# Two attentions and two expert layers in one stream: traced order for loads and gathers, smaller pieces, and another ring of banks for the first attention's turns and projections

## The chip, the core and the metric

The kernel runs on one core of a Trainium2 chip. A core has a matrix engine (TensorE, PE in the profile), a vector engine (VectorE, DVE), a scalar engine for functions of one argument (ScalarE, ACT), a general engine (GpSimd, POOL) and a sync engine (SyncE, SP) from whose queue most DMA transfers are issued. Matrix products land in PSUM, which the kernel uses as eight banks of 128 partitions by 512 floats. The metric is the device time of one execution in microseconds (us), as a median of several runs. A profiled execution, which records every instruction, is longer, and its time is given apart.

## The reference

`x` is 2048 tokens of 128 numbers. Four sublayers are added to it in turn, each fed with a normalization of `x` over its 128 numbers. All is float32.

```
x = x + attention0(layernorm(x))     # 16 heads of 64, all 2048 x 2048 scores, rotary positions
x = x + experts0(layernorm(x))       # 16 experts, the best 2 of 4 groups, the best 4 experts in them
x = x + attention1(layernorm(x))     # 8 heads; each query sees 64 local and 32 chosen positions
x = x + experts1(layernorm(x))       # shared expert + 2 of 8, fixed by the token's number

attention0:  h = layernorm(x) * scale + bias
             q, k, v from two down projections (64 wide) and three up projections; rotary on q and k
             out = softmax(q k^T / 8) v, projected by w_out, + its input
experts0:    s = sigmoid(x Wg); groups by their maximum; weights s / sum(s) * 2.5 of the chosen four
             y = sum_e weight_e * ((silu(x W1_e + b1_e) * (x W3_e + b3_e)) W2_e + b2_e)
attention1:  ckv = x W_dkv (32 wide); index scores I[t,s] = sum_h w_h * relu(qi[t,h] . ki[s])
             idx[t] = the 96 highest of I[t, s <= t], the 64 nearest always among them
             keys, values and a softplus-rotated part are those of ckv and x at idx[t]; softmax over 96
experts1:    y = (shared(x) + (gelu(x W1_a + b1_a) W2_a + gelu(x W1_b + b1_b) W2_b + biases) / 2) / 2
```

## The kernel before

**First attention.** Queries are cut into four groups `g` of 512, heads into eight pairs `pr`; a *unit* is one pair of heads for one group, 32 units in all, group by group. For every unit the scores are computed twice. `by_query` (L264 on) takes 128 queries by 512 keys for both heads: two products `pa` (L275), then a row maximum `mx` on DVE (L280) and exponentials `junk` on ACT (L282) that read the maximum and only keep the row's sum. `close` turns maxima and sums into one reference value and one reciprocal a row, and `turn` (L305 on) transposes the reference values by PE into the row `mrow`. `by_key` (L316 on) computes the transposed scores `pb`, 128 keys by 512 queries (L323), adds the reference by a product of ones with `mrow` (L325), and ACT writes the exponentials `e` (L329). `mean` multiplies them with the compressed values into the accumulator `po` (L338). `project` (L347 on) multiplies `po` with the value and output weights, and DVE adds the result, scaled by the reciprocals, to `xr`, the running `x` of the group.

PSUM is cut into three rings: `ps` with five banks (`pa`, `pb` and the rope's products), `po` with one, `px` with two (all else: `turn`, `project` and everything in the later sublayers). `e` has a ring of seven in SBUF, which the rope's products `t_q`, `t_k` share. `rope` multiplies on DVE (L254) and adds on POOL (L255); keys go to DRAM (`kd`) and come back by two loads a step, `ka` and `kb` (`keys_of`), issued by SP.

**The order.** `run` (L361 on) walks through steps `s`, four to a unit, and in each traces four `by_query`, four `by_key` of the unit before and four `mean` of a step behind that. Between these calls it calls `advance(us)`, 12 us in all in a step. When a group has gone through its eight units, its later sublayers become a *stream*: `follow(g)` is a Python generator that runs `experts0`, `attention1` and `experts1` for the group and yields, after every piece of work, its cost in us. `advance` pulls pieces until their costs have caught up with the time given times `PACE` of that group (L39). So the stream of group `g` is traced between the steps of group `g+1`; the last group's stream has no loop beside it and runs at the end. A stream has about 270 pieces.

Tracing isn't yet the order of execution. A scheduler reorders each engine's instructions by what it takes them to cost and by priority: `mx`, `junk` and `e` are traced with a raised priority (`high_priority(URGENT)`), and `keep_in_program_order` holds single instructions in the order in which they were traced. That order is then fixed for each engine.

**The second attention**, four tiles `n` of 128 queries a group. `index_scores` computes products `pi` of 512 keys (L711), and ACT and DVE build the index scores `v`. `choose` (L733 on) takes the 32 highest of each row by four rounds of maximum, index and replacement on DVE, and turns the indices into `ixT`. Each of 32 *gathers* (L756) then brings one chosen row for 128 partitions from the table in DRAM into `kv`, by an indirect DMA that POOL issues; `pay` (L695) traces them one or a few at a time as the stream's later pieces go by. Eight loads `cl` bring the local windows. `queries` builds the tile's queries. `attend` (L813 on) first rotates the gathered rows, two halves of 16 slots each, four DVE instructions a half (`rotate`, L90 on; the first of them is `rgc`, L95), transposes them (L831), computes scores `pl` (L849 to L855), maximum (L861), exponentials (L865), transposes, and the products with values and output weights (L886 to L907). Slot `2 (g mod 16) + g div 16` takes gather `g`, so the first half holds gathers 0 to 7 and 16 to 23. The tiles are strung together like this:

```
for n in range(4 * g, 4 * g + 4):
    yield from index_scores(n)
    while gathers:
        yield pay(1.8)
    yield from choose(n)
    if pending is not None:
        yield from attend(*pending)
    yield from queries(n)
    pending = (n, self.kv, self.cl, *self.qT)
```

so `attend` of a tile is traced when the next tile has been chosen, and the last one after its own gathers. Both gathers and the multiplications of the gathered rows' rotation are kept in program order.

Of the kernel before, what the change touches and what calls it, by code (L numbers as in the profile page):

```python
# [16 lines left out]
P = 128  # L17
# [21 lines left out]
PACE = (1.0, 1.1, 1.2, 1.2)  # L39
# [24 lines left out]
def layernorm(nc, pool, src, dst, tag):  # L64

    nt = src.shape[1]
    st = pool.tile([P, nt, 6], F32, tag=tag + "st", name=tag + "st")
    mv = pool.tile([P, nt, 2], F32, tag=tag + "mv", name=tag + "mv")
    for n in range(nt):
        nc.vector.bn_stats(st[:, n, :], src[:, n, :])  # L70
        nc.vector.bn_aggr(mv[:, n, :], st[:, n, :])
    v = pool.tile([P, nt], F32, tag=tag + "v", name=tag + "v")
    nc.vector.tensor_scalar(v, mv[:, :, 1], EPS, None, ALU.add)
    r = rsqrt(nc, pool, v, tag)
    for n in range(nt):
        nc.vector.tensor_scalar(
            dst[:, n, :], src[:, n, :], mv[:, n, 0:1], r[:, n : n + 1], ALU.subtract, ALU.mult
        )


def softplus(nc, pool, out, src, one, tag):

    a = pool.tile(list(out.shape), F32, tag=tag + "a", name=tag + "a", bufs=1)
    nc.scalar.activation(a, src, AF.Abs)
    nc.scalar.activation(a, a, AF.Exp, scale=-1.0)
    nc.scalar.activation(a, a, AF.Ln, bias=one)
    nc.vector.scalar_tensor_tensor(out, src, 0.0, a, ALU.max, ALU.add)


def rotate(nc, eng, pool, out1, out2, mu, cos, sin, tag, bufs=None, keep=None):  # L90

    shape = list(mu.shape)
    c = pool.tile(shape, F32, tag=tag + "c", name=tag + "c", bufs=bufs)
    s = pool.tile(shape, F32, tag=tag + "s", name=tag + "s", bufs=bufs)
    first = eng.tensor_tensor(c, mu, bcast(cos, 2, 2), ALU.mult)  # L95
    if keep is not None:
        keep(first)
    second = eng.tensor_tensor(s, mu, bcast(sin, 2, 2), ALU.mult)
    if keep is not None:
        keep(second)  # L100
    eng.tensor_tensor(out1, c[:, :, 0, :], s[:, :, 1, :], ALU.subtract)
    eng.tensor_tensor(out2, s[:, :, 0, :], c[:, :, 1, :], ALU.add)


class Program:
# [23 lines left out]
    def bank(self, name):  # L129

        return self.ps_s.tile([P, 512], F32, tag="ps", name=name)
# [5 lines left out]
    def transposed(self, src, dst, name):  # L137

        pt = self.x(name)
        for j in range(4):  # L140
            self.nc.tensor.transpose(pt[:, j, :], src[:, j, :], self.ident)
        self.nc.scalar.copy(dst, pt.rearrange("p a b -> p (a b)"))

    def prologue(self):
# [40 lines left out]
        for g in range(4):  # L187
            cols = slice(512 * g, 512 * g + 512)
            xn = pp.tile([P, 4, C], F32, tag="xn", name=f"xn{g}", bufs=2)
            layernorm(nc, pp, self.xr[g], xn, "ln0")  # L190
            nc.gpsimd.tensor_tensor(self.xr[g], self.xr[g], xn, ALU.add)
            hn = pp.tile([P, 4, C], F32, tag="hn", name=f"hn{g}", bufs=2)
            layernorm(nc, pp, xn, hn, "ln0")
# [33 lines left out]
        self.ep = self.ctx.enter_context(tc.tile_pool(name="a_e", bufs=7))  # L227
# [77 lines left out]
    def turn(self, u):  # L305

        nc = self.nc
        pm = self.x(f"pt{u}", dtype=BF16)
# [38 lines left out]
    def project(self, u, h):  # L347
# [4 lines left out]
        pm = self.x(f"pp{u}_{h}")  # L352
# [8 lines left out]
    def run(self):  # L361
# [26 lines left out]
        for s in range(4 * NU + BEHIND + 5):  # L388
            u, j = divmod(s, 4)
            ub, jb = divmod(s - BEHIND, 4)  # L390
            um, jm = divmod(s - BEHIND - 1, 4)
            if u < NU and j == 0 and u + 1 < NU:
                self.rope(self.UNITS[u + 1][0], "q", self.UNITS[u + 1][1])
            if u + 1 < 8:
                self.rope(u + 1, "k", j)
            if s == 4 * 8:
                self.keys.close()
            if s + 2 < 4 * NU:
                self.keys_of((s + 2) // 4, (s + 2) % 4, "a")
            sb = s + 2 - BEHIND  # L400
            if 0 <= sb < 4 * NU:
                self.keys_of(sb // 4, sb % 4, "b")
            for half in range(2):
                pair = range(2 * half, 2 * half + 2)
                for i in pair:
                    if 0 <= ub < NU:
                        self.by_key(ub, 4 * jb + i)
                    advance(1.0)
                    if u < NU:
                        self.by_query(u, 4 * j + i)  # L410
                    advance(1.0)
                if half == 1 and u < NU and j == 3:
                    self.close(u)
                for i in pair:
                    if 0 <= um < NU:
                        self.mean(um, 4 * jm + i)
                if half == 0 and j == 0 and 0 <= u - 1 < NU:
                    self.turn(u - 1)
                advance(2.0)
                if jm == 1 and 0 <= um - 1 < NU:  # L420
                    self.project(um - 1, half)
            if jm == 1 and 0 <= um - 1 < NU:
                self.outs.pop(um - 1)
                if um % 8 == 0:
                    if stream is not None:
                        for _ in stream:
                            pass
                    stream, owed, pace = self.follow(um // 8 - 1), 0.0, PACE[um // 8 - 1]
        if stream is not None:
            for _ in stream:  # L430
                pass
# [86 lines left out]
    def experts0(self, sc, g):  # L518
# [6 lines left out]
        layernorm(nc, sm, xr, xn, "ln1")  # L525
        yield 5.0
        xT = sm.tile([P, 512], F32, tag="xT", name=f"xT1_{g}")
        self.transposed(xn, xT, f"pt1_{g}")
        yield 2.0
# [4 lines left out]
        for j in range(4):  # L534
            nc.tensor.matmul(pg[:, j, :], xT[:, j * P : j * P + P], w["wg"], start=True, stop=True)
        s = sm.tile([P, 4, NE0], F32, tag="s", name=f"gs{g}")
# [4 lines left out]
        yield 2.0  # L541
# [3 lines left out]
        def below(v, n, first, k, tag):  # L545
# [3 lines left out]
            eq = sm.tile(shape, F32, tag="eq", name=f"eq{tag}{g}")  # L549
            nc.vector.tensor_tensor(gt, bcast(v, 2, n), bcast(v, 3, n), ALU.is_gt)  # L550
            nc.vector.tensor_tensor(eq, bcast(v, 2, n), bcast(v, 3, n), ALU.is_equal)
            ff = bcast(first.rearrange("p a b -> p (a b)"), 1, 4)
            e2 = eq.rearrange("p t a b -> p t (a b)")
            nc.vector.tensor_tensor(e2, e2, ff, ALU.mult)
            nc.vector.tensor_tensor(gt, gt, eq, ALU.add)
            rank = sm.tile([P, 4, n], F32, tag="rank" + tag, name=f"rank{tag}{g}")
            nc.vector.tensor_reduce(rank, gt, axis=AX.X, op=ALU.add)
            nc.vector.tensor_scalar(rank, rank, float(k) - 0.5, None, ALU.is_lt)
            return rank
# [4 lines left out]
        gsel = below(gm, NG0, w["first4"], 2, "g")  # L564
        yield 3.0
# [6 lines left out]
        esel = below(ms, NE0, w["first16"], 4, "e")  # L572
        yield 7.0
# [13 lines left out]
        yield 2.0  # L587

        pt = self.x(f"ptw{g}", [P, P])
        nc.tensor.transpose(pt, we.rearrange("p a b -> p (a b)"), self.ident)  # L590
        wt = sm.tile([P, P], F32, tag="wt", name=f"wt{g}")
        nc.scalar.copy(wt, pt)
        yield 1.0
        pb = self.x(f"pb2_{g}")
        nc.tensor.matmul(pb.rearrange("p a b -> p (a b)"), wt, w["b2"], start=True, stop=True)
        nc.vector.tensor_tensor(xr, xr, pb, ALU.add)
        yield 1.5


        hs = {}  # L600
        for e in range(NE0 + 1):
            if e < NE0:
                if e + 2 < NE0:
                    wx.append(self.weights(wp, e + 2, f"wb{g}_{e + 2}"))
                hs[e] = self.hidden(hp, wx[e], xT, w["b13"][:, 0, e : e + 1], self.hb[:, e : e + 1], w["b13"][:, 1, e : e + 1], f"b{g}_{e}")
                yield 2.0
            if e > 0:
                h = hs.pop(e - 1)
                py = self.x(f"py{g}_{e}")
                for j in range(4):  # L610
                    nc.tensor.matmul(py[:, j, :], h[:, j * P : j * P + P], wx[e - 1][:, 2, :], start=True, stop=True)
                yield 1.0
                for j in range(4):
                    nc.vector.scalar_tensor_tensor(
                        xr[:, j, :], py[:, j, :], wh[:, j, e - 1 : e], xr[:, j, :], ALU.mult, ALU.add
                    )
                yield 1.0

    def hidden(self, pool, wx, xT, b1, hb1, b3, name):

        nc = self.nc
        p1, p3 = self.x("p1" + name, [P, 512]), self.x("p3" + name, [P, 512])
        nc.tensor.matmul(p1, wx[:, 0, :], xT, start=True, stop=True)  # L623
        nc.tensor.matmul(p3, wx[:, 1, :], xT, start=True, stop=True)  # L624
# [4 lines left out]
        h = pool.tile([P, 512], F32, tag="h", name="h" + name)  # L629
        nc.vector.scalar_tensor_tensor(h, th, 1.0, z, ALU.add, ALU.mult)  # L630
        nc.vector.scalar_tensor_tensor(h, p3, b3, h, ALU.add, ALU.mult)  # L631
        return h

    def attention1(self, sc, g):
# [12 lines left out]
        with ExitStack() as prep:  # L647
            pp = prep.enter_context(tc.tile_pool(name="c_prep", bufs=1, side="right"))
            xn = pp.tile([P, 4, C], F32, tag="xn", name=f"xn2_{g}")
            layernorm(nc, pp, xr, xn, "ln2")  # L650
            yield 5.0
            xT = pp.tile([P, 512], F32, tag="xT", name=f"xT2_{g}")
            self.transposed(xn, xT, f"pt2_{g}")
            yield 2.0
# [3 lines left out]
            for j in range(4):  # L658
                nc.tensor.matmul(pk[:, j, :], xT[:, j * P : j * P + P], w["wck"], start=True, stop=True)
            kg = pp.tile([P, 4, 64], F32, tag="kg", name=f"kg{g}")  # L660
            nc.scalar.copy(kg[:, :, 0:32], pk[:, :, 0:32])
            softplus(nc, pp, kg[:, :, 32:64], pk[:, :, 32:64], self.one, "spk")
            nc.sync.dma_start(table.rearrange("(n p) d -> p n d", p=P)[:, 4 * g : 4 * g + 4, :], kg)
            yield 3.0
# [451 lines left out]
```

## Time and profile before

| | us |
|---|---|
| three runs | 3023.91, 3023.21, 3025.91 (median 3023.91) |
| the profiled execution | 3467.66 |
| its span, first to last instruction | 3465.9 |
| PE busy in the span | 2798.2 (81%) |
| ACT busy | 1739.4 (50%) |
| DVE busy | 1715.1 (49%) |
| POOL busy | 577.9 (17%), of it 491.0 in gathers |
| mean clock granted to PE | 0.861 of full speed |

How to read it: a busy time is the time in which an engine executes instructions; "idle before" is what it stood before a group of instructions, with the event that ended most of that idle time. A line such as `mx<-pa` gives the output and input by the program's names, buffer numbers left out. The clock is a share of full speed. The profiled execution is 443.8 us longer than the median of the runs, so what the profile shows is not all there when nothing is recorded. Before the loop's first `pa` lie 77.8 us of preparation; the loop ends at 2899.7 and the last group's stream at 3465.9. In that tail the last tile's `attend` runs from 3395.9 to 3427.2, and `choose` of tile 12 ends at 3048.0.

### The profile page before, as it was taken

How to read it: one execution, taken by the hardware profiler on the slowest of the kernel's cores; microseconds unless marked ns; L12 is line 12 of the kernel's file. 1: busy time of each engine (PE TensorE's matmuls, PEld its weight loads, DVE VectorE, ACT ScalarE, POOL GpSimd, SP SyncE). 2: the span in 40 equal slices, each digit the busy share in tenths (PEclk: the TensorE clock that was granted, in tenths of full speed). 3: DMA queues.
4: the chain of work that ended last, by engine and by line, in shares of the span. 5: the costliest groups of instructions: out<-in, count | busy, mean ns of one | idle time of the engine just before them, and what ended most of it. 6: DMA issues, size and time to landing. Idle time of an engine off the chain costs nothing. (4 is left out here: it accounts for less than half of the span.)

```text
span 3465.9 us, 38526 instructions
## 1 busy us (share of the span) xinstructions
PE 2798.2 (81%) x13452; PEld 1256.3 (36%) x13452; DVE 1715.1 (49%) x3749; ACT 1739.4 (50%) x4157; POOL 577.9 (17%) x586
## 2 busy tenths in 40 slices
PE   5999999998788899997697899997696877733426
PEld 3444444343233344442243344342242333312214
DVE  7645444565343444665363545555354624664242
ACT  2766667565464566564464466564363542312213
POOL 1111100002313210002312300002303210061330
PEclk7999999999797799998897899997797978856556
DMA  4211111111111111111111111111111101010000
GB/s 130 64 52 52 59 49 38 37 45 33 34 37 27 31 52 38 41 39 28 32 39 28 30 49 43 39 35 28 31 29 25 23 12 42 24 21 5 14 12 26
DMA packets 98097, 127.74 MB, mean 37 GB/s; under 512 B 31344, under 2 KB 49776, under 8 KB 97904
## 3 DMA queue, kind: packets, MB, share of 16 engines
q1 hardware_dynamic: 81520, 108.48, 11.1%
q0 software_dynamic: 16384, 16.81, 2.4%
q8 instruction: 106, 1.74, 0.2%
q14 instruction: 87, 0.71, 0.1%
HBM read 115.26 MB, written 9.96 MB: 36 GB/s over the span
## 5 line engine op out<-in xcount | busy, mean ns | idle before, releaser
L280 DVE TENSOR_REDUCE mx<-pa 128x1 f32<-128x512 f32 x1024 | 673.2, 686 | 695.7 <-PE pa L275 502.3
L282 ACT ACTIVATE junk<-pa,mx 128x512 bf16<-128x512 f32 x1024 | 699.9, 691 | 423.2 <-DVE mx L280 384.5
L275 PE MATMUL pa<-ka,q 64*128 64x512 f32 x2048 | 777.8, 639 | 87.7 <-ACT junk L282 68.2
L329 ACT ACTIVATE e<-pb 128x512 f32<-128x512 f32 x1024 | 556.5, 597 | 473.2 <-PE pb L325 356.2
L323 PE MATMUL pb<-q,kb 64*128 64x512 f32 x2048 | 693.4, 646 | 99.6 <-ACT e L329 73.1
L756 POOL DMA_INDIRECT kv<-table,ixT x512 | 491.0, 959 | 926.1 <-issue 484.2
L338 PE MATMUL po<-e,ckv 128*64 128x512 f32 x2048 | 552.0, 659 | 1.7 <-issue 1.7
L275 PEld LDWEIGHTS pa<-ka,q 64*128 64x128 f32 x2048 | 272.5, 193 | 351.7 <-ACT junk L282 190.3
L323 PEld LDWEIGHTS pb<-q,kb 64*128 64x128 f32 x2048 | 233.7, 193 | 350.9 <-issue 165.6
L255 POOL TENSOR_TENSOR q<-t_q 128x512 f32<-128x512 f32 x32 | 40.7, 1273 | 1560.7 <-DVE t_q L254 1560.7
L325 PE MATMUL pb<-mrow,onesb 64*128 64x512 bf16 x1024 | 262.8, 386 | 2.0 <-issue 1.9
L338 PEld LDWEIGHTS po<-e,ckv 128*64 128x64 f32 x2048 | 133.9, 146 | 348.9 <-issue 337.3
L282 ACT ACTIVATION_READ_ACCUMULATOR junk<-pa,mx 128x1 f32 x1024 | 209.2, 204 | 0.0
L861 DVE TENSOR_REDUCE mx<-pl 128x2 f32<-128x416 f32 x64 | 37.8, 591 | 343.7 <-remote 158.0
L865 ACT ACTIVATE e<-pl,mx 128x208 f32<-128x208 f32 x128 | 54.4, 431 | 242.6 <-DVE mx L862 173.7
L711 PE MATMUL pi<-kiT,qiT 64*128 64x512 f32 (+4 forms) x320 | 123.9, 632 | 47.3 <-issue 17.9
L831 PE MATMUL ptr<-ident,kv 128*128 128x128 f32 x256 | 44.3, 315 | 94.7 <-issue 66.9
L855 PE MATMUL pl<-kr,qT 64*32 64x128 f32 x1024 | 66.9, 320 | 63.6 <-issue 63.5
L325 PEld LDWEIGHTS <-onesb 64*128 64x128 bf16 x1024 | 75.6, 96 | 112.2 <-issue 90.3
L717 DVE SCALAR_TENSOR_TENSOR v<-rl,iw_sb,v 128x512 f32<-128x512 f32 (+4 forms) x120 | 77.1, 644 | 71.9 <-ACT rl L716 64.2
L832 ACT COPY kr<-ptr 128x512 f32<-128x512 f32 x64 | 37.0, 590 | 142.7 <-PE ptr L831 97.0
L630 DVE SCALAR_TENSOR_TENSOR hb<-thb,zb 128x512 f32<-128x512 f32 x64 | 44.3, 692 | 129.4 <-ACT zb L628 127.4
(266 smaller groups left out, 2856.4 us busy)
## 6 DMA issues: line engine op xcount, KB each, us to landing
ka<-kd SPq DMA_DIRECT2D x128, 256.0 KB
kb<-kd SPq DMA_DIRECT2D x128, 256.0 KB
wb<-in_wx SPq DMA_DIRECT2D x64, 192.0 KB
kd<-kst SPq DMA_DIRECT2D x32, 256.0 KB
kv<-table,ixT POOLq DMA_INDIRECT x512
wd<-in_wx SPq DMA_DIRECT2D x40, 192.0 KB
csk<-in_cs SPq DMA_DIRECT2D x4, 512.0 KB
csq<-in_cs SPq DMA_DIRECT2D x4, 512.0 KB
```

Source lines behind the costliest of these rows:

```text
L275: nc.tensor.matmul(ps[h], q[rows, qt * P : qt * P + P], k[rows, :], start=True, stop=True)
L280: nc.vector.tensor_reduce(mx[at], ps[h], axis=AX.X, op=ALU.max, negate=True)
L282: nc.scalar.activation(junk, ps[h], AF.Exp, bias=mx[at], accum_out=su[at])
L323: nc.tensor.matmul(ps[h], k[rows, c], q[rows, :], start=True, stop=False)
L325: nc.tensor.matmul(ps[h], self.onesb[rows, :], mrow[rows, :], start=False, stop=True)
L329: nc.scalar.activation(e[:, h, :], ps[h], AF.Exp)
L338: nc.tensor.matmul(self.pos[u][cols, :], self.ckv[:, kb, :], e[:, h, :], start=(kb == 0), stop=(kb == NT - 1))
L711: nc.tensor.matmul(pi[:, : hi - lo], qiT[h // 2][rows, q], kiT[rows, lo:hi], start=True, stop=True)
L717: nc.vector.scalar_tensor_tensor(v[:, lo:hi], rl[:, : hi - lo], w["iw"][:, h : h + 1], v[:, lo:hi], ALU.mult, ALU.add)
L756: nc.gpsimd.indirect_dma_start(out=kv[:, 2 * (g % 16) + g // 16, :], out_offset=None, in_=table[0 : P * (n + 1), :], in_offset=bass.Indire ...
L855: nc.tensor.matmul(pl[32 * j : 32 * j + 32, c, 80:NK], qs[rows, 32 * gr : 32 * gr + 32], kr[rows, gr % 16, :], start=False, stop=(c == 1),)
L865: nc.scalar.activation(e[:, i, :], pl[:, c, :], AF.Exp, scale=SCALE1, bias=mx[:, i : i + 1], accum_out=su[:, i : i + 1],)
```

## The change

- `manual_schedule` over the engines SP and POOL: both issue their instructions in the order in which they are traced; loads and gathers are no longer placed by the scheduler. `keep_in_program_order` around gathers and rotations goes.
- The later sublayers are cut into more pieces, about 450 a group by the generators' yields, mostly a matrix product or its eviction each. `layernorm`, `softplus`, `rotate`, `transposed` and `hidden` become generators. In `hidden` the product `p3` is traced after the evictions of `p1`, and an expert's output product and addition are traced within the next expert's pieces. `index_scores` is traced so that additions come one piece after the relu that they read. `e` in `attend` is scaled in two halves. `PACE` falls, and a step still advances by 12 us.
- One gather is traced with every piece of `queries` and the following `index_scores` (`paced`). `attend` of a tile and `choose` of the next are merged, one piece of each in turn.
- `turn` and `project` take their banks from the ring of five instead of the ring of two. The ring of `e` has eight buffers.

```diff
-PACE = (1.0, 1.1, 1.2, 1.2)
+PACE = (0.86, 0.93, 1.0, 1.0)
...
-def rotate(nc, eng, pool, out1, out2, mu, cos, sin, tag, bufs=None, keep=None):
+def rotate(nc, pool, out1, out2, mu, cos, sin, tag):
...
+    nc.vector.tensor_tensor(c, mu, bcast(cos, 2, 2), ALU.mult)
+    yield us
+    nc.vector.tensor_tensor(s, mu, bcast(sin, 2, 2), ALU.mult)
+    yield us
+    nc.vector.tensor_tensor(out1, c[:, :, 0, :], s[:, :, 1, :], ALU.subtract)
+    nc.vector.tensor_tensor(out2, s[:, :, 0, :], c[:, :, 1, :], ALU.add)
+    yield us
+
+
+def merge(*parts):
+
+    parts = list(parts)
+    while parts:
+        for p in list(parts):
+            us = next(p, None)
+            if us is None:
+                parts.remove(p)
+            else:
+                yield us
...
-    def bank(self, name):
-
-        return self.ps_s.tile([P, 512], F32, tag="ps", name=name)
+    def bank(self, name, shape=(P, 512), dtype=F32):
+
+        return self.ps_s.tile(list(shape), dtype, tag="ps", name=name)
...
-        self.ep = self.ctx.enter_context(tc.tile_pool(name="a_e", bufs=7))
+        self.ep = self.ctx.enter_context(tc.tile_pool(name="a_e", bufs=8))
...
-        pm = self.x(f"pt{u}", dtype=BF16)
+        pm = self.bank(f"pt{u}", [P, 4, P], BF16)
...
-        pm = self.x(f"pp{u}_{h}")
+        pm = self.bank(f"pp{u}_{h}", [P, 4, C])
...
+        with self.tc.manual_schedule(engines={mybir.EngineType.SP, mybir.EngineType.Pool}):
+            for s in range(4 * NU + BEHIND + 5):
...
+                    for i in pair:
+                        if 0 <= um < NU:
+                            self.mean(um, 4 * jm + i)
+                        advance(1.0)
...
+        last = iter(())
+        for e in range(NE0):
...
+            for k, _ in enumerate(self.hidden(hp, wx[e], xT, *bias, f"b{g}_{e}", h)):
+                if k in (1, 2):
+                    next(last, None)
+                yield 0.8
+            last = output(e, h)
...
-        p1, p3 = self.x("p1" + name, [P, 512]), self.x("p3" + name, [P, 512])
+        p1 = self.x("p1" + name, [P, 512])
         nc.tensor.matmul(p1, wx[:, 0, :], xT, start=True, stop=True)
-        nc.tensor.matmul(p3, wx[:, 1, :], xT, start=True, stop=True)
+        yield
...
+        p3 = self.x("p3" + name, [P, 512])
+        nc.tensor.matmul(p3, wx[:, 1, :], xT, start=True, stop=True)
+        yield
...
-        def pay(us):
-
-            for _ in range(min(len(gathers), max(1, round(us / 1.8)))):
-                gathers.pop(0)()
-            return us
+        def paced(pieces):
+
+            for us in pieces:
+                if gathers:
+                    gathers.pop(0)()
+                yield us
...
-                    tc.keep_in_program_order(
-                        nc.gpsimd.indirect_dma_start(
-                            out=kv[:, 2 * (g % 16) + g // 16, :], out_offset=None, in_=table[0 : P * (n + 1), :],
-                            in_offset=bass.IndirectOffsetOnAxis(ap=ixT[:, g : g + 1], axis=0),
-                        )
+                    nc.gpsimd.indirect_dma_start(
+                        out=kv[:, 2 * (g % 16) + g // 16, :], out_offset=None, in_=table[0 : P * (n + 1), :],
+                        in_offset=bass.IndirectOffsetOnAxis(ap=ixT[:, g : g + 1], axis=0),
                     )
...
-        pending = None
+        last = iter(())
         for n in range(4 * g, 4 * g + 4):
-            yield from index_scores(n)
+            yield from paced(index_scores(n))
             while gathers:
-                yield pay(1.8)
-            yield from choose(n)
-            if pending is not None:
-                yield from attend(*pending)
-            yield from queries(n)
-            pending = (n, self.kv, self.cl, *self.qT)
+                yield from paced(iter((0.8,)))
+            yield from merge(choose(n), last)
+            yield from paced(queries(n))
+            last = attend(n, self.kv, self.cl, *self.qT)
         while gathers:
-            yield pay(1.8)
-        yield from attend(*pending)
+            yield from paced(iter((0.8,)))
+        yield from last
```

## The prediction, made before the changed kernel had been run

> **What bounds the kernel now.** I read the page first (busy times, 40 slices, groups), then busy time by stretch, then the waits and the timeline where the stretches lose time.
>
> From the page of the kernel before:
>
> ```profile
> span 3465.9 us, 38526 instructions
> PE 2798.2 (81%) x13452; PEld 1256.3 (36%) x13452; DVE 1715.1 (49%) x3749; ACT 1739.4 (50%) x4157; POOL 577.9 (17%) x586
> ...
> PEclk7999999999797799998897899997797978856556
> ...
> L756 POOL DMA_INDIRECT kv<-table,ixT x512 | 491.0, 959 | 926.1 <-issue 484.2
> ```
>
> TensorE (PE) is the busiest engine. Its clock is full in the first quarter and falls in three dents and in the last seventh. The 512 gathers take POOL 959 ns each.
>
> Busy time by stretch: a bare stretch of three units, one beside `experts0`, two beside `attention1`, and the tail after the loop (columns: us, then busy us and count per engine):
>
> ```profile
> core 0: us, PE busy (x) PEld busy (x) DVE busy (x) ACT busy (x) POOL busy (x), PEclk, DMA share, GB/s
> 454.90:625.30 170.40, 170.40 (x747) 71.85 (x745) 78.91 (x154) 120.21 (x297) 3.81 (x3) 1.00 0.14 38
> 714.10:797.40 83.30, 83.30 (x379) 37.12 (x376) 53.46 (x139) 55.06 (x123) 1.26 (x1) 1.00 0.15 40
> 889.50:991.20 101.70, 77.98 (x441) 33.48 (x438) 36.09 (x72) 48.95 (x125) 32.56 (x34) 0.83 0.13 32
> 2613.50:2653.50 40.00, 18.22 (x90) 7.60 (x87) 6.35 (x13) 7.11 (x16) 30.26 (x32) 0.72 0.18 39
> 2899.70:3465.90 566.20, 263.79 (x1384) 152.24 (x1383) 260.23 (x485) 121.95 (x261) 122.61 (x128) 0.63 0.08 19
> ```
>
> The bare units are bound by PE: 170.4 of 170.4 us, 56.8 a unit, 3.55 for each of the 16 key blocks. Beside `experts0` PE is still full. Beside `attention1` it is busy 78 of 102 us, and 18 of 40 in a stretch full of gathers, at clock 0.72. The tail (566 us) is a chain of latencies, PE busy under half.
>
> Now how a gather holds everything. Tile 8 is the one tile where the second rotation (`rgc`, L95) came up on VectorE (DVE) before its last gathers. Timeline there (start, duration, then in brackets the idle time before):
>
> ```profile
> 2446.35 0.96 POOL L756 DMA_INDIRECT kv<-table,ixT  x1
> ...
> 2456.48 0.69 DVE L95 TENSOR_TENSOR rgc<-kv,cs 128x512 f32<-128x512 f32 x1 [10.38 <-DMA kv<-table,ixT]
> ...
> 2457.87 0.69 ACT L282 ACTIVATE junk<-pa,mx 128x512 bf16<-128x512 f32 x1 [9.92 <-DVE mx L280]
> ...
> 2458.70 1.22 PE L275 MATMUL pa<-ka,q 64*128 64x512 f32 x1 [6.94 <-issue]
> ```
>
> DVE stood 10.38 us in front of an instruction that waited for gathers; everything behind it stood too, `mx` (L280) first, so ACT lacked `mx`, kept its banks, and PE lost 6.94. So PE rides out 3.4 us of a held DVE, then stops. The last gather needed ended at 2454.9, the rotation began at 2456.5: 1.6 us to land. Gathers start every 1.25 us (2446.35, 2447.62 and so on). The waits (us, times, of which at most in one):
>
> ```profile
> DVE rgc L95 <- DMA kv<-table,ixT: 20.0, 3, 10.4
> ```
>
> Three such cases in all, 20.0 us: first rotations of tiles 0 and 4, second of 8. All others came late enough.
>
> A second thing happens where some twenty gathers have run without a break:
>
> ```profile
> 1676.49 0.95 POOL L756 DMA_INDIRECT kv<-table,ixT  x1 [0.30 <-issue]
> ...
> 1696.51 0.94 POOL L756 DMA_INDIRECT kv<-table,ixT  x1 [0.30 <-issue]
> 1701.29 0.60 ACT L329 ACTIVATE e<-pb 128x512 f32<-128x512 f32 x1 [25.11 <-remote]
> ```
>
> All engines stand, no local releaser is named ("remote"), and go on 4 us after the last gather. The profiled execution took 3467.66 us (span 3465.9), the runs 3023.91: 443.8 us or 27.7 for each of 16 tiles. I take this freeze as the profiler's and absent in the runs.
>
> [...]
>
> **The change, part by part.** The instructions are the same, but for 16 DVE multiplies more (`e` scaled in halves: [...] beside PE work but for the tail: 0). Cost is in order and waits. The orders below are those of the two built programs.
>
> *1. Gathers out of the scheduler's hands, `attend` merged with the next `choose`.* Before, `attend(n)` is traced after `choose(n+1)`; from tile n's index transpose to its first rotation DVE has 21 to 58 maxima over `pa` in tiles 0 to 10. In the changed program, from a tile's first gather to its first rotation DVE has only 4, 4, 5, 4, 4, 6, 6, 6, 5 (tiles 0, 1, 4, 5, 7 to 11): mean 4.9, two to a key block, so 2.45 x 3.55 = 8.7 us of the loop, and some 3 us of stream matmuls among them: 12 us. The first rotation needs gathers 0 to 23 (slots under 16): 24 x 1.25 + 1.6 = 31.6 us. It waits 19.6, PE loses 19.6 - 3.4 = 16.2; nine tiles: 146. The second needs all 32: 41.6. From the first, 10 us later; one key block and the rotation's 2.2 us lie between, it waits 4, of which I count 2 on PE: 18. Tiles 2, 3 and 6 have `q`'s addition (L255) between their gathers. After it 7 gathers are owed in tile 2 (11.6 us with the addition, PE loses 5, and 16 earlier), in tile 3 19 for the first rotation (26.6, less 7 reached and 3.4: 16, and 2), in tile 6 4, then 12 (3 in all): 42. Sum 206. The waits of before (20.0 us, PE about 10) go: +196. Queued behind the waiting rotation: `mx`, then ACT's exponentials, then PE's banks. Bounds: +100 if DVE arrives only 20 us after the first gather, +270 if after 6.
>
> *2. Clock after each of some twelve stops.* [...] +20 (10 to 40).
>
> *3. Tail.* Before, one after the other: `attend` 31 us (tile 15: 3395.9 to 3427.2), `queries` 10, scores 16 to 20, `choose` 24; gathers under `attend`. Now `choose` runs within `attend` (24 + 8 us of DVE), but for tile 13 both rotations stand before the scores of tile 14 on DVE, and `attend` cannot start before its gathers. From `choose(12)`'s end to the kernel's: before 19 + 23, three times (31 + 10), scores 16 + 20, `choose` 24 + 26, 31 and the last stage's 39: 321. After: `choose(13)` ends at 69 (rotation at 42 + 3, then 24 of DVE), gathers to 111, scores to 130, `choose(14)` 162, gathers to 204, scores 212, `choose(15)` 244, gathers 286, `attend` 29, last stage 39: 354. The difference is +33; I take +25 (-35 to +45), as fewer eviction waits help elsewhere.
>
> *4. Smaller pieces, matmul and eviction apart, `px` banks for the streams alone, an `e` ring of 8.* Removes waits in `attention1`. In the profile PE idles 330 us between 625 and 2900; about 190 us of standstill and slow clock are left if I take PE busy time by clock (2367 us with the prologue) from the end of the loop in the runs (3024 - 468, the tail without freezes). `experts0` has nothing to give (PE full). I take a third: -60 (-20 to -130).
>
> *5. `turn` and `project` in the ring of five.* Three more tenants a unit, each held about 3 us (matmul 1.2, four DVE steps 1.1, wait), where `pa` and `pb` hold 3.4 banks on average: +5 (0 to +40).
>
> *6. Loads on SP in traced order.* `ka`, `kb` are traced two steps, 28 us, ahead; an issue takes 0.33 us. What SP queues before them, `cl` and `wx`, waits for matmuls traced earlier: 0, covered by those two steps; uncovered, a key load late by 5 us would cost PE 5 in each of 12 tiles (+60). Lower `PACE`: streams end at step 70, 102, 134 against 69, 101, 133, before the next starts: 0.
>
> Sum: 196 + 20 + 25 - 60 + 5 = +186; 3023.9 + 186 = 3210. In the profile's own account 3467.7 + 186 = 3654, less what waits and freezes share, since both end with the gathers: some 8 us by tile, about 3550.
>
> **Rivals.** *A, the forecast* (3110 to 3310). For it: the case at 2456.5 and the counts of maxima. Against: only three cases in a trace. *B, the freeze is real in the runs too*: the new waits then fall into time already lost; 196 shrinks to about 60, 3024 + 60 + 20 + 25 - 60 + 5: 3075. Against: 443.8 us between profile and runs. *C, faster*: without the profiler the gathers issue quickly. Then 24 of them must be down within the 12 us that DVE needs, one every (12 - 1.6)/24 = 0.43 us; below that no rotation waits, parts 1 and 2 give -10, the tail gains two thirds of three `choose`s (-50), the pieces -60: 2905. Against: 1.25 us at every one of 490 spacings, quiet or busy. *D, no effect* (the scheduler restores the old order): excluded by the orders, but sums can cancel.
>
> **How the numbers follow.** A 0.68, B 0.16, C 0.14, D 0.02. The time is A's. The range reaches from B's side to part 1's upper bound: 3050 to 3330, leaving out C and 2 in 100 above. A measurement of this kernel can tell about 0.2% from no change. Slower 0.83 (A and most of B), same 0.03, faster 0.14.
>
> **What would show it.** Right: `rgc` waits for the `kv` gathers by about 20 us in nine tiles and 4 more at their second rotation, some 200 to 250 us in the chain of waits against 20.0; PE idle "pa" behind it; tile 13's scores after its gathers. Wrong: rotations that wait little; `attention1` units shorter than before; a tail under 500 us with no waits; new idle on `pa` for key loads.

## The result, and the profile after

The changed kernel takes 3359.84 us (median; 3355.55 to 3364.83), the kernel before 3023.56: a ratio of 1.1104, 95% interval 1.1086 to 1.1123. The profiled execution took 3364.83 us. The prediction was 3210, range 3050 to 3330: the direction held, but the time lies 30 us above the range, and the loss of 336 us is nearly twice the 186 that were forecast.

The page of the changed kernel, the lines that answer to those shown of before:

```profile
span 3363.0 us, 38462 instructions
PE 2748.0 (82%) x13452; PEld 1216.9 (36%) x13452; DVE 1702.8 (51%) x3765; ACT 1732.6 (52%) x4157; POOL 575.7 (17%) x586
...
PEclk6999999999888989999779889999879779875556
...
L819 POOL DMA_INDIRECT kv<-table,ixT x512 | 489.0, 955 | 705.0 <-issue 351.9
...
L103 DVE TENSOR_TENSOR rgc<-kv,cs 128x512 f32<-128x512 f32 x32 | 22.3, 696 | 415.7 <-DMA kv<-table,ixT 415.7
```

The first multiplication of a rotation, `rgc`, now waits 415.7 us for gathers, in all 32 rotations; it was 20.0 us in three (22.7 in four in e14). The gathers themselves are as they were (955 ns against 959).

The profile of before in the first part turned out to be a bad ruler: it comes from an execution in which the other engines slowed down or stood while gathers ran, and the timed runs were not like that (see e1 and e14). That a profiled execution is longer, as the first part says, hardly holds here: in e14 it takes 3026.74 us beside a median of 3021.99. e14 profiled the kernel before on a chip where it takes these 3022 us. Busy time there in the loop from the first unit that has a stream beside it, and in the tail (us of the stretch, then busy us and count of each engine, clock, DMA):

```profile
core 0: us, PE busy (x) PEld busy (x) DVE busy (x) ACT busy (x) POOL busy (x), PEclk, DMA share, GB/s
624.90:2557.60 1932.70, 1832.55 (x9576) 813.22 (x9571) 1106.59 (x2456) 1222.05 (x2931) 395.76 (x405) 0.96 0.15 40
2557.60:3025.00 467.40, 258.20 (x1384) 150.44 (x1383) 260.58 (x485) 122.31 (x261) 127.36 (x128) 0.65 0.09 23
```

The same two stretches of the changed kernel, same columns:

```profile
635.50:2862.50 2227.00, 1869.69 (x9500) 790.11 (x9495) 1095.50 (x2461) 1213.52 (x2923) 392.17 (x405) 0.90 0.13 35
2862.50:3363.00 500.50, 279.85 (x1460) 163.55 (x1459) 259.27 (x495) 129.13 (x270) 123.43 (x128) 0.63 0.09 21
```

This is where the 338 us between the two profiled executions (3363.0 and 3025.0) lie. The loop is 294.3 us longer: PE's idle time there went from 100.2 to 357.3 (+257), and its busy time from 1832.6 to 1869.7 (+37), at a mean clock of 0.90 against 0.96. The tail is 33.1 longer; 76 matrix products more lie in it than before (1460 against 1384). The remaining 10.6 lie before that unit. The other trace of the changed kernel, e5, reaches the unit at 624.3 us, as early as before, so this part is put down to the one execution.

How one tile loses it: tile 4, timeline of the changed kernel.

```profile
1588.03 0.96 POOL L819 DMA_INDIRECT kv<-table,ixT  x1 [16.56 <-DMA cl<-table]
...
1600.18 1.94 PE L364 MATMUL po<-e,ckv 128*64 128x512 f32 x8
...
1619.61 0.69 DVE L103 TENSOR_TENSOR rgc<-kv,cs 128x512 f32<-128x512 f32 x1 [23.16 <-DMA kv<-table,ixT]
...
1620.99 0.69 ACT L308 ACTIVATE junk<-pa,mx 128x512 bf16<-128x512 f32 x1 [22.72 <-DVE mx L306]
...
1623.28 2.07 PE L754 MATMUL pi<-kiT,qiT 64*128 64x512 f32 x2 [21.15 <-ACT qT L871]
...
1629.70 0.69 DVE L103 TENSOR_TENSOR rgc<-kv,cs 128x512 f32<-128x512 f32 x1 [7.38 <-DMA kv<-table,ixT]
...
1633.67 1.22 PE L754 MATMUL pi<-kiT,qiT 64*128 64x512 f32 x1 [8.32 <-ACT qT L871]
```

VectorE comes to the rotation at 1596.4 (1619.61 less the wait), 8.4 us after the first gather's start (1588.0), and stands 23.16 us. PE goes on until 1602.1 with what it has, then stands 21.15. Ten us later the second rotation waits 7.38 for the last eight gathers, and PE stands 8.32 behind it. Over the twelve tiles of the loop the first rotations wait 254 us and the second ones 82.

### The profile page after: what moved, and what is told of

The parts are those of the page before. It is cut to its first block, busy times and chain, and to the rows that moved or that the text cites. A ratio compares the mean times of both kernels' runs of the same rounds, so it can differ in the third digit from the quotient of the medians.

```text
span 3363.0 us, 38462 instructions
## 1 busy us (share of the span) xinstructions
PE 2748.0 (82%) x13452; PEld 1216.9 (36%) x13452; DVE 1702.8 (51%) x3765; ACT 1732.6 (52%) x4157; POOL 575.7 (17%) x586
## 5 line engine op out<-in xcount | busy, mean ns | idle before, releaser
L301 PE MATMUL pa<-ka,q 64*128 64x512 f32 x2048 | 741.2, 637 | 176.2 <-ACT junk L308 169.6
L349 PE MATMUL pb<-q,kb 64*128 64x512 f32 x2048 | 637.1, 639 | 33.2 <-ACT junk L308 18.8
L301 PEld LDWEIGHTS pa<-ka,q 64*128 64x128 f32 x2048 | 257.0, 192 | 440.6 <-ACT junk L308 290.1
L349 PEld LDWEIGHTS pb<-q,kb 64*128 64x128 f32 x2048 | 215.4, 190 | 274.5 <-issue 117.6
L351 PE MATMUL pb<-mrow,onesb 64*128 64x512 bf16 x1024 | 245.0, 383 | 0.0
L103 DVE TENSOR_TENSOR rgc<-kv,cs 128x512 f32<-128x512 f32 x32 | 22.3, 696 | 415.7 <-DMA kv<-table,ixT 415.7
L867 PE MATMUL ptq<-ident,qq 128*128 128x128 f32 x256 | 47.7, 331 | 90.5 <-ACT qT L871 46.0
L383 DVE SCALAR_TENSOR_TENSOR xr<-pp,rs,xr 128x128 f32<-128x128 f32 x256 | 72.8, 344 | 72.7 <-PE pp L380 72.7
L754 PEld LDWEIGHTS pi<-kiT,qiT 64*128 64x128 f32 x320 | 52.2, 231 | 143.5 <-DVE v L773 50.8
L759 ACT ACTIVATE rl<-pi 128x512 f32<-128x512 f32 (+4 forms) x120 | 58.7, 516 | 84.3 <-PE pi L754 72.9
```

The costliest lines, as they stand in the source:

```text
L301: nc.tensor.matmul(ps[h], q[rows, qt * P : qt * P + P], k[rows, :], start=True, stop=True)
L349: nc.tensor.matmul(ps[h], k[rows, c], q[rows, :], start=True, stop=False)
L351: nc.tensor.matmul(ps[h], self.onesb[rows, :], mrow[rows, :], start=False, stop=True)
L383: nc.vector.scalar_tensor_tensor(xr[:, j, :], pm[:, j, :], self.rs[u][:, j, h : h + 1], xr[:, j, :], ALU.mult, ALU.add)
L754: nc.tensor.matmul(pi, qiT[h // 2][rows, q], kiT[rows, lo:hi], start=True, stop=True)
L759: nc.scalar.activation(rl, pi, AF.Relu)
```

## The experiments

The chips were not alike. On some, the kernel before takes 3023 us, as in the comparison; on others its median is 3428 to 3455. Each run below is set against the kernel before on its own chip, and that time is given. "A chip that slows" means one of the second kind.

**Theory 1:** the loss is VectorE standing before rotations that were placed ahead of their gathers. **Theory 2:** the smaller pieces, the banks or SP's order make it. **Theory 3:** the gathers hold the chip, wherever VectorE stands.

**e1, e14: the kernel before, profiled again.**

> The kernel before, unchanged, profiled once more. If the 443.8 us between its profiled execution and its runs are what recording costs, the new span is again near 3460 us with all engines standing for 14 to 25 us behind long rows of gathers. If that one execution was a disturbed one, the span is near 3022 us, the engines go on during the gathers, and the loop ends near 2560 us instead of 2899.7. The profiled execution of the changed kernel, whose span (3363.0) is its own run's time, speaks for the second.

> The kernel before, for its profile. If it runs at about 3023 us here, the loop ends near 2560 us, PE is near 100% beside gathers, and no engine stands in rows of gathers except for VectorE before three rotations; the tail takes about 465 us.

Measured: e1 3446.3 us, and 3449.18 (15 runs) for the kernel before beside it; e14 3021.99, beside 3024.77. So the long execution in the first part was no effect of recording, since e14 is recorded too and spans 3025.0 us; nor a single disturbance, since e1's chip shows it in every run. It goes with the chip, or with the hour, since each chip was seen in one session only. Away from gathers the two kinds are alike: the first unit with a stream beside it begins at 624.9 us in e14 and at 625.3 in the first profile, in which gathers slow PE too. The same row of 32 gathers (the last nine of tile 4 and 23 of tile 5), busy times in e14:

```profile
1530.20:1569.50 39.30, 38.05 (x174) 15.42 (x173) 16.86 (x28) 26.81 (x66) 29.83 (x32) 1.00 0.21 53
```

and in e1:

```profile
1650.70:1690.50 39.80, 16.87 (x59) 5.56 (x55) 6.66 (x11) 9.10 (x23) 30.20 (x33) 0.73 0.16 39
```

With the gathers going at the same pace, PE does 38.05 us of work in 39.3 on the one chip and 16.87 in 39.8 on the other. The timeline of e1 within another row shows PE's instructions coming slowly one by one, with no event that they would wait for ("issue"):

```profile
1165.63 0.18 PEld L323 LDWEIGHTS pb<-q,kb 64*128 64x128 f32 x1 [1.53 <-issue]
...
1166.35 0.37 PE L325 MATMUL pb<-mrow,onesb 64*128 64x512 bf16 x1
...
1167.76 0.10 PEld L325 LDWEIGHTS <-onesb 64*128 64x128 bf16 x1 [1.82 <-issue]
1168.46 0.58 PE L325 MATMUL pb<-mrow,onesb 64*128 64x512 bf16 x1 [1.70 <-issue]
```

**e2, e7, e13: the changed kernel with the rotations held.**

```diff
-    nc.vector.tensor_tensor(c, mu, bcast(cos, 2, 2), ALU.mult)
+    keep(nc.vector.tensor_tensor(c, mu, bcast(cos, 2, 2), ALU.mult))
...
-    nc.vector.tensor_tensor(s, mu, bcast(sin, 2, 2), ALU.mult)
+    keep(nc.vector.tensor_tensor(s, mu, bcast(sin, 2, 2), ALU.mult))
```

`keep` is `tc.keep_in_program_order` for the gathered rows and nothing elsewhere.

> The changed kernel, with the two multiplications of each rotation of gathered rows held in program order again, as before. In the order of instructions their place moves from 4 to 34 maxima behind the index transpose to 8 to 46, which is where PE's transposes of the rows want them. Theory 1 (VectorE standing before gathers makes the loss): the waits of rgc for gathers fall from 415.7 us to under 130 (the tail's 80 stay) and the time from 3360 to about 3080 us (3020 to 3140). Theory 2 (smaller pieces, banks or SP's order make the loss): above 3290. Theory 3 (the gathers themselves hold the chip, wherever VectorE stands): above 3290 too, with waits moved to other instructions.

> The changed kernel with the rotations held, once more, to be set against the unchanged one on one chip. Where gathers don't slow the others, theory 1 gives 2960 to 3080 us (the plain load gave 2943) and theory 2 (pieces, banks, SP's order) above 3290; where they do, it stays near 3470 as in the first run of it, since nothing but the place of the loss is changed.

> The changed kernel with real gathers and the rotations held in program order. If before runs at about 3023 us here, theory 1 gives 2960 to 3050 (stand-ins with the hold gave 3019, the plain load 2943), with waits of rgc under 40 us in the loop; theory 2 over 3250. If before runs at about 3450, about 3475 as in its first two runs.

Measured: e2 3472.68 us beside 3449.18 (ratio 1.0063, 1.0043 to 1.0083), e7 3477.11 beside 3454.79 (1.0082, 1.0049 to 1.0114), both on chips where gathers slow PE. e13, on one where they don't: 3041.22 beside 3024.77 (1.0052, 1.0034 to 1.0071), as theory 1 expected. Where gathers leave PE alone, the hold gives back 319 of the 336 us. On a chip that slows it gives nothing back: e7 is 29 us longer than the unheld kernel on the same chip (e5, below). Waits of the rotations in e13 (us, times, longest):

```profile
DVE rgc L103 <- DMA kv<-table,ixT: 67.4, 9, 12.7
```

Of these, 34 us lie in the loop, where it was 336. The two stretches of e13, to be set against those of the changed kernel above; the number of products in each is the same:

```profile
623.80:2563.60 1939.80, 1828.93 (x9500) 770.24 (x9496) 1094.60 (x2461) 1212.83 (x2923) 400.40 (x405) 0.96 0.15 40
2563.60:3027.20 463.60, 259.89 (x1460) 154.76 (x1459) 259.20 (x495) 128.22 (x270) 125.80 (x128) 0.67 0.09 23
```

Without the waits the loop is 287 us shorter: PE is idle for 110.9 instead of 357.3 and busy for 1828.9 instead of 1869.7, and the tail is 37 shorter. The loop's mean clock is 0.96 (0.90 in the changed kernel, 0.96 in e14). So the hold takes away the lost clock and the tail's loss as well as the idle time.

In the order of instructions one sees why. The table counts the maxima `mx` on VectorE and the products `pa` on PE from the start of the loop, two to a key block:

| tile | index transpose after maximum | first rotation, changed | first rotation, held | PE's transposes after product |
|---|---|---|---|---|
| 0 | 392 | 396 | 400 | 412 |
| 4 | 648 | 653 | 660 | 670 |
| 5 | 664 (held 668) | 676 | 704 | 710 |
| 9 | 928 (held 930) | 934 | 960 | 970 |

PE's transposes stand at the same place in both kernels. Nobody needs the rotated rows before them, so the early rotations served nothing. If the merge of `choose` and `attend` alone is undone in the changed program, tile 4's 5 maxima and tile 9's 6 between index transpose and rotation stay as they are. It is the dropped hold, not the merge, that moved them. (That is its order alone; it was not run.)

**e3, e4: one plain load in place of a tile's gathers.**

```diff
-            gathers.extend(gather(g) for g in range(32))
+            nc.sync.dma_start(
+                kv.rearrange("p r d -> p (r d)"),
+                table[0:RK, :].rearrange("r d -> (r d)").unsqueeze(0).to_broadcast([P, RK * 64]),
+            )
```

> The changed kernel, with the 32 gathers of a tile replaced by one plain load of 32 fixed rows to all partitions from SP; the choice of rows is left out of what is computed, all other work stays. Theory 1: no rotation waits over 5 us in the loop, the loop's loss and the tail's 80 us of waits go, and the time is about 2970 us (2880 to 3060). Theory 2: the loop keeps its loss, only the tail gains some 60: about 3290 us. Theory 3: about 2970 as in theory 1, so the next kernel tells 1 and 3 apart.

> The kernel before, with the same replacement of the gathers; the choice of rows is left out of what is computed. Theory 1: gathers cost the kernel before little, the three waits of 20 us and part of those in the tail: 2960 us (2920 to 3010). Theory 3: gathers hold the kernel before as well: under 2880.

Measured, both on a chip that slows: the changed kernel 2942.89 us (2935.89 to 2947.85), the kernel before 3012.17 (3007.28 to 3013.68; 2 us above what was expected), beside 3449.18. All that such a chip adds hangs on the gathers: 437 us for the kernel before. On the other chips its gathers cost some 12 us (3024 against 3012), those of the changed kernel some 417 (3360 against 2943), if the kernels with the plain load take as long there. Without gathers the changed kernel is faster by 69 us on one chip, of which 66 lie in the tail (392.8 us after the loop against 459.0) and 5 in the loop (1921.7 against 1927.1).

**e5, e6, e8, e19: on chips that slow.** e5 is the changed kernel as it is; e6 and e19 are the kernel before without the hold of the rotations (`tc.keep_in_program_order` dropped from the call); e8 is the changed kernel with `self.x` for `self.bank` in `turn` and `project`.

> The changed kernel, unchanged, beside the kernel before on whatever chip this is. The last runs gave 3449 us for the kernel before where the comparison had 3023.6, and the profile shows PE at two thirds while gathers run; in the profile of the changed kernel PE was full beside 20 gathers (24.70 of 24.70 us, clock 1.00). If the gathers of this chip slow the other engines (before at about 3450), the waits of the changed kernel fall into time that is lost anyway: 3360 to 3480. If they don't (before at about 3023), 3360 as before.

> The kernel before, with nothing changed but that the rotations of gathered rows are no longer held in program order. In the order of instructions, tiles 8 to 11 then have 5, 10, 6 and 6 maxima between index transpose and rotation (21, 54, 39, 6 before), the others 15 to 44. Theory 1 (the hold alone decides whether VectorE stands before gathers): waits of rgc of about 20 us in each of tiles 8 to 11, and before's time + 50 to 90 us where gathers don't slow the others; where they do, within 30 us of before. Rival (it takes the new cutting and the merge): waits and time as before.

> The changed kernel with the turns and projections of the first attention back in the ring of two. Prediction: the ring of five costs 5 us, so 5 less than the changed kernel (40 less at most). Rival (sharing px with the streams was a brake that the change took away): 10 to 60 us more than the changed kernel.

> The kernel before with the rotations of gathered rows no longer held in program order, once more. Where before runs at about 3023 us: tiles 8 to 11 come to their first rotation 5 to 10 maxima after the index transpose and wait about 20 us there, and the tail's rotations wait too, so theory 1 gives 3080 to 3150 us; the rival (the new cutting is needed for the loss) 3010 to 3040. Where before runs at about 3450: within 20 us of it, as in its first run.

Measured: e5 3447.96 us beside 3454.79 (0.997, 0.9954 to 0.9987); e6 3460.51 (1.0023, 1.0007 to 1.0038); e8 3456.03 (1.0006, 0.9984 to 1.0028), 8 more than e5; e19 3449.77 beside 3427.74 (1.006, 1.0042 to 1.0078). On such a chip the changed kernel is not slower at all. In e6 and e19 the rotations wait 209.9 and 226.7 us without any of the new cutting, where the changed kernel on e6's chip (e5) waits 260.0. Dropping the hold is thus enough for most of the waits, though not in each of the tiles that were expected: in e6, tiles 8 and 9 wait some 20 us at their first rotation, tiles 10 and 11 under 5. What these waits would cost where gathers leave PE alone was not tried.

**e9, e10, e11: the gathers' time without their DMA.**

```diff
-                    nc.gpsimd.indirect_dma_start(
...
+                    nc.gpsimd.tensor_tensor(pad, pad, pad, ALU.add)
+                    nc.gpsimd.tensor_copy(kv[:, 2 * (g % 16) + g // 16, :], ixT[:, g : g + 1].to_broadcast([P, 64]))
```

e10 has the hold of e2 besides, e11 is the kernel before with the same stand-ins, in program order.

> The changed kernel with each gather replaced by two POOL operations (an addition on 380 numbers a partition that does nothing useful, then a copy into the same slot of kv) that take about as long as a gather, 1.2 us, and wait for the same index transpose; the choice of rows is left out of what is computed. It keeps the order and the time of the gathers and takes their DMA away. VectorE's order is the changed kernel's (4 to 32 maxima between index transpose and rotation). Theory 1 (VectorE stands before what POOL has not delivered): rotations wait some 20 and 7 us a tile and the time is the 2943 us of the plain load + 300 to 420: 3300 (3240 to 3370). If the waits cost little by themselves: under 3050.

> The same stand-ins in the changed kernel with the rotations held in program order. Theory 1: rotations no longer wait in the loop, 2970 us (2930 to 3050). Theory 2 (something else in the changed kernel, such as its rows of POOL work in traced order): within 50 us of the kernel with stand-ins and free rotations.

> The same stand-ins in the kernel before. If the first comparison's chip let gathers run without harm to the other engines, this is its 3024 us again: 3000 to 3050 (the plain load gave 3012).

Measured beside 3023.07 us: e9 3268.18 (3264.16 to 3272.66), e10 3019.45 (3008.92 to 3030.82), e11 3053.13 (3046.56 to 3060.78). Waits of the rotations, in e9:

```profile
DVE rgc L103 <- POOL kv L822: 276.0, 28, 38.9
```

and in e10:

```profile
DVE rgc L103 <- POOL kv L822: 20.1, 1, 20.1
```

With no gather in the kernel, POOL's delay alone makes a loss of 245 us, and the hold takes 249 us away on the same chip. A stand-in took 0.95 us instead of 1.25, so both waits and loss are smaller than with gathers: 276.0 us of waits against 415.7, 325 us over the plain load (on another chip) against 417. e11 is 3 us above what was expected for it. With e13, which keeps the pieces, the banks, SP's order and the gathers themselves, this settles theory 1 against 2 and 3 for chips like that of the comparison.

**e12, e20, e21: the small terms.** e12 is e3 with `turn` and `project` back in `px`; e20 the kernel before with them in the ring of five; e21 the kernel before with `manual_schedule` over SP and POOL.

> The changed kernel with the plain load in place of gathers, and turns and projections back in the ring of two; without gathers the banks' part can be seen. Prediction: 5 us less than the plain load alone (2943), at most 40 less. Rival (the ring of two was a brake): 5 to 60 us more.

> The kernel before with turns and projections in the ring of five, nothing else. The prediction: 5 us slower (0 to 40). The runs with the plain load (2959 against 2943 us) say the other way: 10 to 20 us faster than before, which would beat both kernels.

> The kernel before with SP and POOL issuing in traced order, nothing else; POOL's order is the same in both, so this is SP's loads. The prediction: 0 us, at most 60 more if key loads come late. Rival (loads in traced order come late behind cl and wx): 10 to 60 us more, with idle time before pa for ka.

Measured: e12 2959.3 us (2951.61 to 2965.7) against e3's 2942.89, on different chips, but both without gathers; e20 3430.82 beside 3427.74 (1.0001, 0.9982 to 1.002); e21 3432.81 (1.0011, 0.9991 to 1.0032), these two on a chip that slows. The ring of five gains about 16 us without gathers, if the two chips are otherwise alike, and 8 on one chip in the changed kernel (e8 against e5); in the kernel before, on a chip that slows, it isn't seen. SP's order costs nothing that can be seen there.

**e15: a gap between gathers.** The held kernel of e2 with `nc.gpsimd.tensor_tensor(pad, pad, pad, ALU.add)` before each gather.

> The changed kernel with the rotations held and a useless POOL addition on 380 numbers a partition before each gather, so that gathers start every 2.1 us instead of 1.25. Where gathers leave PE alone: as without the additions, plus some 60 us in the tail (four tiles, 32 x 0.85 us less what is hidden): 3000 to 3110. Where they slow it: if the slowing comes from gathers without a gap, under 3300; if from their number, 3450 to 3560.

Measured 3253.1 us beside 3024.77 (1.0738, 1.0706 to 1.0771): a miss, by 140. In the loop gathers started every 1.97 us, so a row takes 63 us, about as long as tile 5 has between index transpose and PE's transposes (42 products, 75 us) and longer than tiles 0 and 4 have (20 and 22 products, some 40 us). VectorE waits 175.3 us before rotations again, and PE's transposes wait 106.9 for VectorE. In the tail there was no gap to test: 42 of the additions ran in one block ahead of tile 12's first gather (41 us), which held that tile's first rotation for 48.0 us. The chip was one on which gathers leave PE alone, so the run says nothing on the others.

## Why the prediction went wrong

**The mechanism was right.** "`rgc` waits for the `kv` gathers by about 20 us in nine tiles and 4 more at their second rotation": in those nine tiles they wait 22.5 and 6.9 us on average. The "wrong" signs (rotations that wait little, shorter `attention1` units, a tail under 500 us with no waits, new idle time for key loads) stayed away. What failed is the size of several terms. Of the 150 us that are missing, some 61 lie in part 1 and 60 in part 4.

**Part 1, +196, was too small:** PE's idle time in the loop rose by 257 us. The first term that failed is the 12 us that VectorE was to need from the first gather. It took 8.9 on average in the nine tiles (6.6 to 11.8), as the count of maxima alone would give (8.7), without the 3 us that were added for stream products. The second is the wait of the second rotation, put at 4 us with half of it counted: it is 6.9, and PE had little in hand by then (in tile 4 it stood 8.32 behind a wait of 7.38). These two account for up to 26 and 44 us. The 3.4 us that PE rides out fits on average: 336 us of waits in 24 rotations made 257 us more idle time, 3.3 less for each. The part also gave two causes for one: by the order of instructions the merge is innocent.

**Part 2, +20:** PE's busy time grew by 37 us, or by 41 against e13 with the same 9500 products. The 20 were an estimate of the author's, given without working. There were 24 waits instead of some twelve stops, 1.7 us for each. In tile 4 the granted clock was 1.00 ahead of the stops (1590 to 1602), 0.50 for the first products behind the stop of 21.15 us (1623.3 to 1625.4), 0.50 and then 0.55 behind that of 8.32 (1633.7 to 1637.4), and 1.00 again from 1637.5 to 1640.4.

**Part 3:** the addition gave +33 and 25 was taken; the tail grew by 33. That the addition agrees is in part luck. From the end of `choose(12)` to the kernel's end it had 321 us before and 354 after; measured are 319 (e14) and 339, so +20. The steps between are close (`choose(13)`, `(14)` and `(15)` end at 63, 158 and 239 instead of 69, 162 and 244). The other 13 us lie ahead of `choose(12)`'s end.

**Part 4, -60, is the other large error.** It took 190 us of PE's standstill and slow clock to be left in the runs, from a profile in which gathers slowed PE, and counted a third of them as gained. Nothing of the kind is seen in the loop: with the plain load it gains 5 us, and with the rotations held PE is idle for 110.9 us against 100.2 before (e13, e14). Why smaller pieces gain so little in the loop stays open. The 66 us that the new order gains in the tail with the plain load are not there with gathers: e13's tail is 4 us shorter than e14's.

**Part 5, +5,** has the wrong sign in e8 (8 us gained) and e12 (16, across two chips), while e20 shows no difference. **Part 6, 0,** stands as far as e21 can show.

Put together as measured: 257 + 37 + 33 and the 10.6 of the one execution's start, 338 us.

**The freeze.** The prediction took it for the profiler's, which no trace showed. It is neither that nor absent in runs: it goes with the chip (e1, e14). Rival B, the freeze real in the runs too, is thus what happens on chips that slow, and further than it was put: there the new waits fall altogether into time that is lost anyway, and the ratio is 0.997 (e5) instead of 1.02. Rival C asked for gathers faster than 0.43 us; in every trace where they follow each other without additions they start every 1.25 us.

## What to carry to other kernels

A scheduler may place an instruction long before anyone needs its result. If what it waits for comes late, the engine stands, and so does what comes behind it in the engine's order: in tile 4 VectorE stood 23.16 us before a rotation, ACT 22.72 for the maximum behind it, and PE 21.15. Here a hold on two instructions of each rotation is worth 319 us where gathers leave PE alone, and nothing where they slow it. Before estimating a gain from idle time, make sure that the profile is of an execution that took the time one wants to explain: 444 us between profile and runs was a question to be answered first, not a number to be put down to recording.

## What was not expected of the hardware

The same program takes 3023 us on some chips and 3428 to 3455 on others, steadily within each (3438 to 3471 in 15 runs of e1's chip). The difference hangs on gathers that POOL issues: with one plain load in their place the kernel before takes 3012 us on a chip of the second kind. There, mostly some 12 to 25 us into a row of gathers, PE's instructions come one to two us apart, or not at all for some 20 us until 3 to 6 us after the last gather in most rows, while gathers keep their pace of 1.25 us. In the row of e1 above the last gather ended at 1690.7, and PE, after 22.20 us of standing, went on at 1696.0. What in the chip does this, and whether gaps between gathers would avoid it, stays open.
